# Handing out an attention kernel's side work in smaller portions, one step apart

## The chip, the cores and the metric

The kernel runs on one NeuronCore of a Trainium2 chip as one program in one launch. The metric is the device time in microseconds (us); the time of a kernel is the median of its runs. The engines are TensorE (PE; PEld is its weight load), VectorE (DVE), ScalarE (ACT), GpSimd (POOL) and SyncE (SP), which issues most of the DMAs. All data are fp32.

## The reference

Two layers work on x of 4 images, 32 x 32 tokens, 384 channels. The change lies in layer 0, in its attention and in the routing that follows it. Layer 0, cut to what matters:

```
qkv = layernorm(x) @ qkv_w.T;  q, k, v split into 12 heads of 32
attn = softmax(q @ k.T * 32**-0.5)
gidx = argmax(q @ gp)                  # each token picks one of 48 groups, per head
q_mean = mean of q over each group
tidx = top_k(q_mean @ k, 96)           # per group: its 96 best tokens
col = how many groups of the head chose token m
attn = attn * col;  attn = attn / (attn.sum(over n) + 1e-8)
x = x + (attn @ v) @ proj_w.T
p = softmax(layernorm(x) @ gate_w + gate_b);  the best 2 of 4 experts, weights made to sum to 1
x = x + sum over them of weight * (gelu(layernorm(x) @ w1 + b1) @ w2 + b2)
```

Layer 1 (a local attention over 3 x 3 windows and a feed-forward block) comes after it and is not touched.

## The kernel before

The attention is one long software pipeline. There are 48 heads (4 images of 12) and four steps (u = 0 to 3) a head, so 192 steps; a step treats two tiles of 128 keys against all 1024 queries. The order of the work on PE, DVE, ACT and SP is written out by hand: what Python emits first, an engine runs first. POOL's order is left to the compiler. In each step the loop emits, in this order:

- `scores(u)` (PE, L627) into two PSUM buffers `ps_s`, and `exps` (ACT, L637), which empties them into `e`;
- `out` of eight steps before (PE, L645 into `ps_o`; it needs that step's `wv`), and `total` of one step before (PE, L645 into `ps_z`);
- at u = 0 `gather` of the head before: ACT copies its sums `zr` (L659), SP writes them to DRAM (`z_row`, L661) and reads them back in another layout (`zz`, L663); at u = 3 `keep`: ACT copies a finished head's `po` (L709), SP writes one half over `q` (L718), and POOL's DMA adds the other (`q<-po`, L716);
- `begin` (functions that earlier steps put off with `later`), `widen` (starts a search), for the image before its projection and its routing, the values, then preparation (`prepared`) as far as a budget of 2.6 us a step goes;
- `share` of seven steps before (DVE, L689: two passes over `e` with the row `rz`; then `d` and `wv`, L694 and L696);
- at u = 1 `spread` of the head before: DVE makes `rr` from `zz` (L671, L673), SP writes it (`r_row`, L675) and reads it back to all partitions (`rz`, L677);
- `search()`, `end()`, `search()`: the running searches go on by one portion each time; `end` runs what waits in `ends`, for instance `choose` and a projection's sum;
- at u = 1 the next `Head`: eight DMAs on SP copy its q and k into `q4` and `k4` (L614, L615), which have two buffers each.

The side work is written as Python generators; a `yield` ends a portion. `topk` is the search for the 96th best score of 128 rows: an ACT pass for the size (L366), eight rounds of an ACT pass with Sign (L373) and a new bound by DVE (L377, L379), an exact end by DVE over two halves of the row (L383 to L407), one more Sign (L411) and its use (L413, then `count` one step later). Up to two searches run at once; one starts each 9.4 steps. `prepare` does an image's statistics (BN_STATS, L482 and L483; `std`, L487), normalization, transposes and its q and k. `groups` chooses each token's group (`choose`, L555 and L557), counts the choices (`tally`, ACT, L565) and sums q by group (PE, L589). `prepare` and `groups` yield a cost and a condition; a unit runs once the condition holds. `after(1)` holds from the next step on.

`routed` calculates an image's routing during the next image's heads, one portion a step from its 27th step on; `route` ranks the experts (L1306 to L1325), counts tokens (PE, L1339 and L1340), makes slots and weights (L1342 to L1363) and scatters token numbers into a table (POOL, L1374). After image 2 `router.first` finds the rows of the first four expert blocks, whose weights (L1577) and tokens are then fetched. Image 3's routing and `schedule` run beside the first expert blocks.

Of the kernel before, what the change touches and what calls it, by code (L numbers as in the profile page):

```python
# [23 lines left out]
NH, HD = 12, 32  # L24
# [134 lines left out]
def attention(net, outer, router, x, x1, unsafe, qkv_wT, gpT, proj_wT, proj_w, gate_w, gate_b):  # L159
# [15 lines left out]
    NHEAD = B * NH  # L175
# [8 lines left out]
    with ExitStack() as ctx:  # L184
# [161 lines left out]
        def topk(b, t):  # L346
# [59 lines left out]
            nc.vector.scalar_tensor_tensor(between[:n], last[:n], -(1 - 2.0**-23), none[:n], ALU.mult, ALU.subtract)  # L406
            nc.vector.tensor_scalar(own[:n], hsel[:n, t, :], none[:n], 2.0, ALU.mult, ALU.mult)  # L407
            yield
            over = small("tk_over")
            sign = left.bitcast(BF)[:, :NTOK]  # L410
            nc.scalar.activation(sign[:n], left[:n], AF.Sign, bias=between[:n], accum_out=over[:n])  # L411
# [38 lines left out]
        def prepare(b):  # L450

            im = images[b]
            yield 0, lambda: b == 0 or b - 1 in valued
            xnT = im["xnT"] = early.tile([P, KC, NTOK], FP, name="xnT", tag="xnT")
            for name in ("col", "inv"):
                im[name] = tiny.tile([P, NB, NH], FP, name=name, tag=name, bufs=2)
            nc.gpsimd.memset(im["col"], float(NG))  # L460
            im["mean"] = few.tile([P, NB], FP, name="mean", tag="mean", bufs=3)
            im["std"] = few.tile([P, NB], FP, name="std", tag="std", bufs=3)
            im["z"] = tiny.tile([P, NH, NB], FP, name="zall", tag="zall", bufs=1)
            im["x"] = few.tile([P, NB, NE], FP, name="gate_x", tag="gate_x", bufs=3)

            def turn(xn, o):
                ps = psum()
                for c in range(KC):
                    nc.tensor.transpose(ps[:, c * P : (c + 1) * P], xn[:, c * P : (c + 1) * P], net.ident)
                nc.scalar.copy(xnT[:, :, o : o + P], ps[:, :C].rearrange("p (c t) -> p c t", c=KC))  # L470

            behind = []
            for half in range(2):
                if half and b:
                    yield 0, after(2)
                xt = xts.pop((b, half))
                mv = tiny.tile([P, 4, 2], FP, name="ln_mv", tag="ln_mv", bufs=2)
                rs = tiny.tile([P, 4], FP, name="ln_rs", tag="ln_rs", bufs=2)
                off = tiny.tile([P, 4], FP, name="ln_off", tag="ln_off", bufs=2)
                for t in range(4):  # L480
                    st = tiny.tile([P, 6], FP, name="ln_st", tag="ln_st", bufs=2)
                    nc.vector.bn_stats(st, xt[:, t, :])  # L482
                    nc.vector.bn_aggr(mv[:, t, :], st)  # L483
                    if t % 2:
                        yield 0.3, None
                std = im["std"][:, 4 * half : 4 * half + 4]
                nc.scalar.activation(std, mv[:, :, 1], AF.Sqrt, bias=net.eps["c"])  # L487
                yield 0.3, after(1) if b else None
                nc.vector.tensor_copy(im["mean"][:, 4 * half : 4 * half + 4], mv[:, :, 0])
                nc.vector.reciprocal(rs, std)  # L490
                nc.vector.scalar_tensor_tensor(off, mv[:, :, 0], -1.0, rs, ALU.mult, ALU.mult)
                for two in range(2):

                    yield 1.8, after(1) if b else None
                    while behind:
                        turn(*behind.pop(0))
                    for t in (2 * two, 2 * two + 1):
                        xn = work.tile([P, C], FP, name="xn", tag="xn")
                        nc.scalar.activation(
                            xn, xt[:, t, :], AF.Identity, bias=off[:, t : t + 1], scale=rs[:, t : t + 1]  # L500
                        )
                        behind.append((xn, (4 * half + t) * P))
                if half == 0 and b:
                    fetch(b, 1)
                elif half and b + 1 < B:
                    if b == 0:
                        gating()
                    fetch(b + 1, 0)
            yield 1.8, after(1) if b else None
            while behind:  # L510
                turn(*behind.pop(0))
            for c in range(KC):
                yield 0, lambda: (
                    (b == 0 or len(heads) > NH * (b - 1) + 4 * c + 3)
                    and (b < 2 or len([p for p in projected if p[0] == b - 2]) == NB)
                )
                q = lasting.tile([P, NTOK], FP, name="q", tag="q", bufs=6)
                k = big.tile([P, NTOK], FP, name="k", tag="k", bufs=3)
                im["q"].append(q)
                im["k"].append(k)  # L520
                for out, base in ((q, 0), (k, C)):
                    for half in range(2):
                        yield 2.6, None
                        cols = slice(half * 512, half * 512 + 512)
                        ps = psum()
                        o = base + c * P
                        linear(ps, lambda k: wqkv[:, k, o : o + P], lambda k: xnT[:, k, cols])
                        nc.scalar.copy(out[:, cols], ps)
                reached.add((b, c, "qk"))

        def groups(b):

            im = images[b]
            for c in range(KC):
# [28 lines left out]
                def tally(two, ones_):  # L563
                    one = NB // 2 * (KC * b + c) + two
                    nc.scalar.activation(ones_, ones_, AF.Copy, accum_out=onehot[:, one : one + 1])  # L565
                    chosen.append(two)

                for two in range(NB // 2):
                    yield 0.7, lambda: not ends
# [201 lines left out]
        def routed(b):  # L771
# [24 lines left out]
            yield from router.route(b, logit, im["mv"][:, :, 0], rs)  # L796
            if b == B - 2:
                yield
                router.first()
            if b == B - 1:  # L800
                yield
                yield from router.schedule(late[0])
# [60 lines left out]
        for step in range(STEPS + OUT + 2):  # L863
# [39 lines left out]
            search()  # L903
            end()
            search()
            if u == 1 and n + 1 < NHEAD:
                heads.append(Head(n + 1))
        residue(B - 1, 0)
        assert not ends and not others
# [305 lines left out]
class Router:  # L1215
# [71 lines left out]
    def route(self, b, logit, mean, rs):  # L1287
# [18 lines left out]
        nc.vector.tensor_reduce(one, prob, AX.X, ALU.add)  # L1306
        nc.vector.reciprocal(one, one)
        nc.vector.tensor_tensor(prob, prob, all_(one), ALU.mult)
        pairs = [P, NB, NE, NE]
        ge, gt = self.temp("ge", pairs), self.temp("gt", pairs)  # L1310
        other = prob.unsqueeze(2).to_broadcast(pairs)
        mine = prob.unsqueeze(3).to_broadcast(pairs)
        for t, op, mask in ((ge, ALU.is_ge, self.lower), (gt, ALU.is_gt, self.upper)):
            nc.vector.tensor_tensor(t, other, mine, op)
            nc.vector.tensor_tensor(t, t, mask.unsqueeze(1).to_broadcast(pairs), ALU.mult)
        nc.vector.tensor_tensor(ge, ge, gt, ALU.add)
        sel, at = self.sel[:, tiles, :], self.at[:, tiles, :]
        nc.vector.tensor_reduce(sel, ge, AX.X, ALU.add)
# [24 lines left out]
        nc.vector.tensor_tensor(self.upto[:, b + 1, :], self.upto[:, b, :], pc[:, NE : 2 * NE], ALU.add)  # L1343
        nc.vector.tensor_tensor(base, base, self.region, ALU.add)
        nc.vector.tensor_tensor(at, src, base.unsqueeze(1).to_broadcast(wide), ALU.add)

        part = self.temp("part", wide)
        big = float(2 * NE * NT * P)
# [4 lines left out]
        nc.vector.tensor_scalar(slot[0], slot[0], -1.0, big, ALU.mult, ALU.add)  # L1353
        nc.vector.tensor_tensor(part, at, sel, ALU.mult)
        nc.vector.tensor_reduce(slot[1], part, AX.X, ALU.max)
        there = []
        for n in range(2):
            i = self.temp(f"there_{n}", [P, NB], mybir.dt.int32)
# [23 lines left out]
    def first(self):  # L1382

        nc = self.nc
        shape = [P, NE, self.NJ]
        full = self.temp("full", [P, NE])
        nc.vector.tensor_scalar(full, self.upto[:, B - 1, :], -float(XB), None, ALU.add)
        fills = self.temp("gt", shape)
        nc.vector.tensor_tensor(
            fills, full.unsqueeze(2).to_broadcast(shape), self.steps.unsqueeze(1).to_broadcast(shape), ALU.is_ge  # L1390
        )
        nc.vector.tensor_reduce(full, fills, AX.X, ALU.add)

        self.start = self.pool.tile([P, B + 2, NE], FP, name="rt_start")
        self.begun = self.pool.tile([P, B + 2, NE], FP, name="rt_begun")
        nc.gpsimd.memset(self.begun[:, 0, :], 0.0)
        pre = self.start[:, 0, :]
        nc.gpsimd.memset(pre[:, 0:1], 0.0)
        for e in range(1, NE):
            nc.vector.tensor_tensor(pre[:, e : e + 1], pre[:, e - 1 : e], full[:, e - 1 : e], ALU.add)  # L1400
        taken = self.begun[:, 1, :]
        nc.vector.tensor_scalar(taken, pre, -1.0, float(NFIRST), ALU.mult, ALU.add)
        nc.vector.tensor_scalar(taken, taken, 0.0, None, ALU.max)
        nc.vector.tensor_tensor(taken, taken, full, ALU.min)
        nc.vector.tensor_scalar(taken, taken, float(UNITS), None, ALU.mult)
        nc.vector.tensor_scalar(pre, pre, float(NFIRST), float(UNITS), ALU.min, ALU.mult)
        self.firsts = self.rows(self.pool, "first", NFIRST, 1)

    def rows(self, pool, name, n, groups):
# [883 lines left out]
def metaformer_kernel(  # L2293
# [65 lines left out]
    with tc.If(tc.nc.values_load(unsafe[0:1, 0:1], min_val=0, max_val=1) != 0):  # L2359
        with ExitStack() as outer:  # L2360
# [4 lines left out]
            with ExitStack() as inner:  # L2365
                router = routing(inner)
                for b, given in enumerate(gates(net, router.psum, gate_w, gate_b)):
                    for _ in router.route(b, *given):
                        pass
                    if b == B - 2:  # L2370
                        router.first()
                done = experts(net, router, x1, x2, wup, wdown, router.schedule)
        rest(router, done)

# [58 lines left out]
```

## Time and profile before

| | us |
|---|---|
| median of 3 runs | 2778.15 (2777.52 to 2788.7) |
| the profiled execution's own time | 2777.38 |
| its span, first to last instruction | 2774.9 |

| stretch of the span, us | stage | PE busy | DVE busy | ACT busy | granted clock |
|---|---|---|---|---|---|
| 0 to 80 | loads, first preparation | 54.32 | 14.27 | 30.01 | 1.00 |
| 80 to 1127 | attention, heads 0 to 45 | 962.28 | 757.09 | 793.46 | 0.94 |
| 1127 to 1206 | last heads, end of the pipeline | 51.49 | 52.45 | 24.14 | 0.74 |
| 1206 to 2250 | experts | 1030.15 | 533.18 | 203.76 | 1.00 |
| 2250 to 2775 | layer 1 | 467.21 | 371.29 | 250.49 | 0.94 |

The granted clock is the share of TensorE's full speed that the throttle let through. In a line of waits, the first name is the engine and instruction that stood idle, the name after `<-` is what ended that, and then come the sum in us, the number of times and the longest. A line of the timeline gives the start, the duration, engine, source line, operation and tiles, and in brackets the idle time before it.

### The profile page before, as it was taken

To read this page: it belongs to the slowest core of one execution; us is meant where nothing else is said; L and a number is where in the kernel's file an instruction comes from. 1 tells how busy PE (TensorE), PEld (TensorE's weight loads), DVE (VectorE), ACT (ScalarE), POOL (GpSimd) and SP (SyncE) were. 2 spreads that over 40 slices of the span, in tenths; PEclk is the share of its full clock that TensorE was granted. 3 is DMA by queue.
4 is the path that set the end of the run, shared out by engine and by line. 5 is a ranking of instruction groups with operands and counts; after the bars stand their busy time and mean duration, and the time that the engine had idled before them with its cause. 6 is when DMAs were issued, how large, how long until landed. Compare 5 with 4: busy or idle time off the path is not lost. (4 is left out here: it accounts for less than half of the span.)

```text
span 2774.9 us, 40133 instructions
## 1 busy us (share of the span) xinstructions
PE 2565.5 (92%) x14667; PEld 1558.3 (56%) x14667; DVE 1728.3 (62%) x4362; ACT 1301.9 (47%) x2119; POOL 417.8 (15%) x501
## 2 busy tenths in 40 slices
PE   6889999999999998789999999999999987999988
PEld 3323333333333332247889999999999953555532
DVE  1367778677778787647444544465455556887962
ACT  3778777677778777412221221121121123455455
POOL 1000000030003001413211112222222101110000
PEclk9989999999999998889999999999999999999989
DMA  5133434322322232454665545655655447565532
GB/s 108 33 103 92 108 86 126 95 60 63 96 73 64 59 107 69 133 175 160 230 238 207 202 170 216 232 194 217 237 205 211 175 145 221 165 201 175 173 110 93
DMA packets 215806, 404.13 MB, mean 146 GB/s; under 512 B 83344, under 2 KB 176848, under 8 KB 202544
## 3 DMA queue, kind: packets, MB, share of 16 engines
q1 hardware_dynamic: 184496, 187.82, 22.6%
q0 software_dynamic: 26960, 209.05, 22.0%
q10 hardware_dynamic: 4144, 4.61, 0.5%
q8 instruction: 118, 1.93, 0.3%
q14 instruction: 88, 0.72, 0.1%
HBM read 304.34 MB, written 49.00 MB: 127 GB/s over the span
## 5 line engine op out<-in xcount | busy, mean ns | idle before, releaser
L1702 ACT ACTIVATE h<-ps_h,up 128x256 f32<-128x256 f32 (+1 forms) x420 | 195.1, 465 | 825.3 <-PE ps_h L1697 823.7
L1697 PE MATMUL ps_h<-xbT,up 128*128 128x256 f32 (+1 forms) x2520 | 531.1, 371 | 2.5 <-ACT h L1702 1.8
L689 DVE CUSTOM_DVE_ANT_0 e<-e,rz,inv 128x1024 f32<-128x1024 f32 x384 | 475.3, 1274 | 47.3 <-DMA rz<-r_row 47.3
L1697 PEld LDWEIGHTS ps_h<-xbT,up 128*128 128x128 f32 x2520 | 462.6, 191 | 64.6 <-ACT h L1702 2.6
L637 ACT ACTIVATE e<-ps_s,ten 128x1024 f32<-128x1024 f32 x384 | 408.0, 1109 | 66.6 <-PE ps_s L627 40.1
L627 PE MATMUL ps_s<-q,k 32*128 32x512 f32 x1536 | 297.4, 671 | 51.5 <-ACT e L637 35.0
L645 PE MATMUL ps_o<-e,wv 128*32 128x512 f32 x1536 | 227.2, 666 | 40.3 <-DVE wv L696 38.8
L716 POOL DMA_DIRECT2D q<-po x96 | 76.2, 886 | 947.6 <-DMA q<-po 452.9
L645 PE MATMUL ps_z<-e,rt_ones 128*32 128x512 f32 x1536 | 217.1, 639 | 0.0
L373 ACT ACTIVATE below<-tk_left,tk_bound 128x1024 bf16<-128x1024 f32 (+1 forms) x160 | 184.4, 1152 | 52.4 <-DVE tk_bound L379 41.4
L1741 PE MATMUL ps_y<-wsum,hsum 128*128 128x192 f32 x1116 | 196.0, 329 | 9.5 <-DVE hsum L1657 5.2
L627 PEld LDWEIGHTS ps_s<-q,k 32*128 32x128 f32 x1536 | 92.8, 191 | 189.1 <-ACT e L637 92.0
L1741 PEld LDWEIGHTS ps_y<-wsum,hsum 128*128 128x128 f32 x1116 | 182.5, 191 | 13.2 <-DVE hsum L1657 6.6
L1881 PE MATMUL ps_a<-wa,xnT 128*128 128x486 f32 x384 | 162.1, 571 | 0.6 <-ACT xnT L156 0.6
L1745 DVE TENSOR_TENSOR y<-ps_y,y 128x192 f32<-128x192 f32 x155 | 55.5, 358 | 165.5 <-PE ps_y L1741 162.4
L645 PEld LDWEIGHTS ps_o<-e,wv 128*32 128x32 f32 x1536 | 31.5, 112 | 201.0 <-issue 66.1
L288 PE MATMUL ps_t<-xnT,wqkv 128*128 128x512 f32 x288 | 134.6, 607 | 2.4 <-ACT xnT L470 1.7
L1541 POOL DMA_INDIRECT yt<-yg,index x64 | 78.1, 1220 | 375.5 <-DVE x L1844 181.4
L645 PEld LDWEIGHTS ps_z<-e,rt_ones 128*32 128x32 f32 x1536 | 52.2, 117 | 132.0 <-issue 128.8
L1741 PE MATMUL ps_y<-down,h 128*128 128x192 f32 x744 | 126.0, 326 | 0.0
L1741 PEld LDWEIGHTS ps_y<-down,h 128*128 128x128 f32 x744 | 122.6, 190 | 1.6
L1991 ACT COPY own<-band 128x1040 f32<-128x1040 f32 x96 | 101.7, 1125 | 33.2 <-DMA band<-room 30.8
(398 smaller groups left out, 3576.7 us busy)
## 6 DMA issues: line engine op xcount, KB each, us to landing
band<-room SPq DMA_DIRECT2D x32, 1560.0 KB
rz<-r_row SPq DMA_DIRECT2D x48, 512.0 KB
yg<-y SPq DMA_DIRECT2D x67, 192.0 KB
q<-q SPq DMA_DIRECT2D x192, 64.0 KB
k<-k SPq DMA_DIRECT2D x192, 64.0 KB
room<-none SPq DMA_DIRECT2D x64, 192.0 KB
x<-x SPq DMA_DIRECT2D x35, 192.0 KB
o<-in_x_dram SPq DMA_DIRECT2D x33, 192.0 KB
```

The lines of the kernel that those rows point to most:

```text
L288: nc.tensor.matmul(ps, lhsT=lhsT(k), rhs=rhs(k), start=k == 0, stop=k == KC - 1)
L373: nc.scalar.activation(junk[:n], left[:n], AF.Sign, bias=bound[:n], accum_out=over[:n])
L627: nc.tensor.matmul(ps[:, half * 512 : half * 512 + 512], lhsT=self.k4[r, u * P : (u + 1) * P], rhs=self.q4[r, :], start=True, stop=True,)
L637: nc.scalar.activation(e, ps, AF.Exp, bias=shift, scale=QK_SCALE)
L645: nc.tensor.matmul(ps[r : r + 32, :], lhsT=lhsT(odd), rhs=self.es[2 * u + odd][:, half * 512 : half * 512 + 512], start=u == 0, stop=u == ...
L689: nc.vector.tensor_tensor_reduce(self.es[m], self.es[m], self.rz, 1.0, self.im["inv"][:, m, self.h : self.h + 1], ALU.mult, ALU.add, self. ...
L1541: self.nc.gpsimd.indirect_dma_start(out=y, out_offset=None, in_=self.net.yg[: first_row(self.complete(i // NB)), :], in_offset=bass.Indire ...
L1697: nc.tensor.matmul(ps, lhsT=up[:, o : o + P], rhs=xbT[:, k, :size], start=k == 0, stop=k == KC - 1,)
L1702: nc.scalar.activation(hs[f // 3][:, f % 3, :size], ps, AF.Gelu, bias=up[:, KC * HID + f : KC * HID + f + 1])
L1741: nc.tensor.matmul(ps, lhsT=left[f], rhs=right[:, f, :], start=f == 0, stop=f == HF - 1)
L1881: nc.tensor.matmul(pa[:, :HW_], lhsT=xnTs[i][:, k, :], rhs=wa[:, k, hh * HW_ : (hh + 1) * HW_], start=k == 0, stop=k == KC - 1,)
L1991: nc.scalar.copy(own[:, pairs], m.rearrange("p t (n h) -> p n t h", h=2)[:, pairs])
```

## The change

Nothing is added to or taken from the computation; portions are cut and moved.

1. `topk` yields once more before its last Sign.
2. In `prepare`, for images 1 to 3, two tiles' statistics are one portion, and the next comes in a later step.
3. `tally` reports its choice one step later, so the group sums start one step later.
4. `route` yields four more times, and `router.first` becomes a generator of three portions.
5. The next `Head` is made at the end of step u = 0 if its q and k are there, else at u = 1 as before.

```diff
--- before.py
+++ after.py
@@ -406,6 +406,7 @@
             nc.vector.scalar_tensor_tensor(between[:n], last[:n], -(1 - 2.0**-23), none[:n], ALU.mult, ALU.subtract)
             nc.vector.tensor_scalar(own[:n], hsel[:n, t, :], none[:n], 2.0, ALU.mult, ALU.mult)
             yield
+            yield
             over = small("tk_over")
             sign = left.bitcast(BF)[:, :NTOK]
             nc.scalar.activation(sign[:n], left[:n], AF.Sign, bias=between[:n], accum_out=over[:n])
@@ -482,7 +483,7 @@
                     nc.vector.bn_stats(st, xt[:, t, :])
                     nc.vector.bn_aggr(mv[:, t, :], st)
                     if t % 2:
-                        yield 0.3, None
+                        yield 0.3, after(1) if b else None
                 std = im["std"][:, 4 * half : 4 * half + 4]
                 nc.scalar.activation(std, mv[:, :, 1], AF.Sqrt, bias=net.eps["c"])
                 yield 0.3, after(1) if b else None
@@ -563,7 +564,7 @@
                 def tally(two, ones_):
                     one = NB // 2 * (KC * b + c) + two
                     nc.scalar.activation(ones_, ones_, AF.Copy, accum_out=onehot[:, one : one + 1])
-                    chosen.append(two)
+                    later(lambda: chosen.append(two))
 
                 for two in range(NB // 2):
                     yield 0.7, lambda: not ends
@@ -796,7 +797,7 @@
             yield from router.route(b, logit, im["mv"][:, :, 0], rs)
             if b == B - 2:
                 yield
-                router.first()
+                yield from router.first()
             if b == B - 1:
                 yield
                 yield from router.schedule(late[0])
@@ -903,7 +904,7 @@
             search()
             end()
             search()
-            if u == 1 and n + 1 < NHEAD:
+            if u < 2 and len(heads) == n + 1 < NHEAD and (u or ((n + 1) // NH, (n + 1) % NH // 4, "qk") in reached):
                 heads.append(Head(n + 1))
         residue(B - 1, 0)
         assert not ends and not others
@@ -1306,6 +1307,7 @@
         nc.vector.tensor_reduce(one, prob, AX.X, ALU.add)
         nc.vector.reciprocal(one, one)
         nc.vector.tensor_tensor(prob, prob, all_(one), ALU.mult)
+        yield
         pairs = [P, NB, NE, NE]
         ge, gt = self.temp("ge", pairs), self.temp("gt", pairs)
         other = prob.unsqueeze(2).to_broadcast(pairs)
@@ -1313,6 +1315,7 @@
         for t, op, mask in ((ge, ALU.is_ge, self.lower), (gt, ALU.is_gt, self.upper)):
             nc.vector.tensor_tensor(t, other, mine, op)
             nc.vector.tensor_tensor(t, t, mask.unsqueeze(1).to_broadcast(pairs), ALU.mult)
+        yield
         nc.vector.tensor_tensor(ge, ge, gt, ALU.add)
         sel, at = self.sel[:, tiles, :], self.at[:, tiles, :]
         nc.vector.tensor_reduce(sel, ge, AX.X, ALU.add)
@@ -1343,6 +1346,7 @@
         nc.vector.tensor_tensor(self.upto[:, b + 1, :], self.upto[:, b, :], pc[:, NE : 2 * NE], ALU.add)
         nc.vector.tensor_tensor(base, base, self.region, ALU.add)
         nc.vector.tensor_tensor(at, src, base.unsqueeze(1).to_broadcast(wide), ALU.add)
+        yield
 
         part = self.temp("part", wide)
         big = float(2 * NE * NT * P)
@@ -1353,6 +1357,7 @@
         nc.vector.tensor_scalar(slot[0], slot[0], -1.0, big, ALU.mult, ALU.add)
         nc.vector.tensor_tensor(part, at, sel, ALU.mult)
         nc.vector.tensor_reduce(slot[1], part, AX.X, ALU.max)
+        yield
         there = []
         for n in range(2):
             i = self.temp(f"there_{n}", [P, NB], mybir.dt.int32)
@@ -1390,6 +1395,7 @@
             fills, full.unsqueeze(2).to_broadcast(shape), self.steps.unsqueeze(1).to_broadcast(shape), ALU.is_ge
         )
         nc.vector.tensor_reduce(full, fills, AX.X, ALU.add)
+        yield
 
         self.start = self.pool.tile([P, B + 2, NE], FP, name="rt_start")
         self.begun = self.pool.tile([P, B + 2, NE], FP, name="rt_begun")
@@ -1404,6 +1410,7 @@
         nc.vector.tensor_tensor(taken, taken, full, ALU.min)
         nc.vector.tensor_scalar(taken, taken, float(UNITS), None, ALU.mult)
         nc.vector.tensor_scalar(pre, pre, float(NFIRST), float(UNITS), ALU.min, ALU.mult)
+        yield
         self.firsts = self.rows(self.pool, "first", NFIRST, 1)
 
     def rows(self, pool, name, n, groups):
@@ -2368,7 +2375,8 @@
                     for _ in router.route(b, *given):
                         pass
                     if b == B - 2:
-                        router.first()
+                        for _ in router.first():
+                            pass
                 done = experts(net, router, x1, x2, wup, wdown, router.schedule)
         rest(router, done)
```

The last hunk belongs to a second path, taken only where the first one's method doesn't fit the data; it isn't executed here.

## The prediction

> **What bounds the kernel now.** I read the page's slices first, then busy time and clock by stage, then who waited for whom in the stage of the change, then single stalls in the timeline.
>
> ```profile
> PE   6889999999999998789999999999999987999988
> ACT  3778777677778777412221221121121123455455
> PEclk9989999999999998889999999999999999999989
> ```
>
> Attention fills the first 17 slices. TensorE is at 9 there, but not full, with dips in the clock row. By stage (window, length, PE, PEld, DVE, ACT, POOL busy, granted clock, DMA):
>
> ```profile
> 80.00:1127.00 1047.00, 962.28 (x6172) 335.78 (x6171) 757.09 (x2222) 793.46 (x1212) 123.46 (x136) 0.94 0.32 83
> 1127.00:1206.00 79.00, 51.49 (x303) 12.88 (x299) 52.45 (x143) 24.14 (x27) 18.68 (x20) 0.74 0.40 116
> 1206.00:2250.00 1044.00, 1030.15 (x5497) 941.43 (x5497) 533.18 (x1081) 203.76 (x430) 231.93 (x232) 1.00 0.56 206
> ```
>
> In 80:1127 (nearly all heads) PE is idle for 1047 - 962 = 85 us, and the missing 6% of clock is worth another 0.06 x 1047 = 63 us. So some 148 us lie there beyond PE's own work. The experts stage (99% busy, clock 1.00) leaves nothing. PE's waits in 80:1127 (us, times, longest):
>
> ```profile
> PE ps_s L627 <- ACT e L637: 35.0, 22, 4.7
> PE ps_o L645 <- DVE wv L696: 20.5, 12, 4.6
> PE ps_t L589 <- ACT g L565: 8.8, 8, 1.4
> PE ps_s L627 <- DMA k<-k: 7.5, 9, 2.9
> ```
>
> All waits of that answer make 84.4 us. Why is ACT late with e? In the same window ACT itself waits:
>
> ```profile
> ACT below L373 <- DVE tk_bound L379: 40.9, 27, 6.3
> ACT tk_left L411 <- DVE tk_parts L406: 36.8, 15, 5.8
> ```
>
> One such place in the timeline, and the clock before and after it:
>
> ```profile
> 311.03 1.15 ACT L411 ACTIVATE tk_left<-tk_left,tk_parts 64x1024 bf16<-64x1024 f32 x1 [3.11 <-DVE tk_parts L406]
> 312.18 1.13 ACT L373 ACTIVATE below<-tk_left,tk_bound 128x1024 bf16<-128x1024 f32 x1
> 313.31 2.09 ACT L637 ACTIVATE e<-ps_s,ten 128x1024 f32<-128x1024 f32 x2
> 314.46 3.08 PE L627 MATMUL ps_s<-q,k 32*128 32x512 f32 x8 [2.72 <-ACT e L637]
> 306.50:314.46 7.96, 5.07 (x29) 1.38 (x25) 7.44 (x29) 4.85 (x8) 1.56 (x2) 1.00 0.44 87
> 314.46:321.42 6.96, 6.96 (x33) 1.76 (x34) 3.35 (x10) 5.54 (x7) 0.00 (x0) 0.52 0.24 59
> ```
>
> ACT stands 3.11 us before the search's last Sign (L411), with another Sign and the next two exps queued behind; the exps free the score banks late, and PE stands 2.72 us. Then the clock is 0.52 for 7 us, so those 7 us hold 3.5 us of work. One 3 us wait costs 6 us.
>
> **The change part by part**, against the profiled execution (2777.38 us; span 2774.9).
>
> *Extra yield before the last Sign.* The Sign stood behind DVE's second half of the search (two instructions of 0.7 us, nine small ones); now it goes into the next step, behind that step's exps. No instruction is added. Thirteen PE waits between 99.9 and 1121.0 us follow an L411 wait within 9 us. Taking the smaller of the two each time: 2.2, 2.2, 2.7, 3.2, 1.0, 2.6, 0.8, 0.9, 1.2, 0.7, 0.7, 1.2, 3.0 = 22.4 us. What comes late next is DVE's L413, which now waits in the same step; behind it stands the next step's share (L689). The nearest row is DVE's wait at L377 for a Sign, 63.5 us in 38, so 20 x 1.7 = 34 us of DVE idle time, at 72% busy. Bounds: 0 to 34 x (22.4 / 36.8) = 21 us of PE; I take 0 because few of the L377 waits are followed by a PE wait.
>
> *Statistics in pairs one step apart (images 1 to 3).* Four BN_STATS with aggregation (4 x (0.53 + 0.18) = 2.8 us) lay in one step, now 1.4. Five PE waits follow such a step (1.4 to 3.7 us at 145.4, 176.0, 180.0, 424.9, 459.0): 5 x 1.4 = 7.0 us at most. Preparation ends up to four steps later per image; the steps near 925 us (4.1 us each against a usual 5.7) have no preparation left, so that is covered. Uncovered it would be four steps, 16 us an image.
>
> *Group sums one step after the tally.* The 8.8 us of L589 <- L565 go; PE does a preparation unit instead. If that delays a search, it is by one step of a schedule of 9.4 steps each.
>
> *Routing and first() in pieces.* L1306 to L1325 is 15 DVE instructions, 4.1 us, in one step; L1342 to L1363 is 18, 3.1 us. DVE's share comes behind them and PE's out is due in the next step: waits of 2.6, 1.6, 0.7 and 1.7, 1.7, 4.6 us. Pieces shorten the first burst by 2 us or more, the second by 2.5: 2.0 + 1.6 + 0.7 + 1.7 + 1.7 + 2.5 = 10.2 us. DVE's wait for PE's counts (L1342 <- L1340, 9.5 us) stays. The 16 table scatters (1.26 us each on POOL) move four steps later, past q<-po DMAs; the scatters of 1104 to 1128 already held one up, and ACT waited 1.8 us for it (L709). Bounds -2 to +5 us; I take 0, since as many are passed as before. Image 3's routing runs beside the experts: it needs 27 of the 30 portions that blocks 0 to 2 hand out instead of 23, so its end stays in block 2, at no cost.
>
> *Heads one step earlier.* Eight q/k DMAs on SP (0.6 us of issue each) go before r_row and rz of the head before, and before the x loads and stores of the next step. Their buffers were freed by the scores of the step before, so they wait for nothing new:
>
> ```profile
> 606.89 0.37 SPq L663 DMA_DIRECT2D zz<-z_row  x1
> 609.11 0.33 SPq L675 DMA_DIRECT2D r_row<-rr  x1
> 610.51 0.32 SPq L677 DMA_DIRECT2D rz<-r_row  x1
> 616.16 0.63 SPq L615 DMA_DIRECT2D k<-k  x1
> ```
>
> Gained: the 7.5 us of L627 <- DMA k. Added: the eight issues last from zz at 606.89 + 0.4 to 612.3, so r_row goes 3.2 us later than 609.11. For all 46 heads with this rule, rz (1.45 us behind r_row, landing 4.2 us after issue) would land after DVE's share started in 26 of them, together 44 us; minus the time by which wv was early for PE, 6 us of PE wait stay. Bounds 6 to 44; I take 6, because it is worked out head by head.
>
> *After 1127.* PE stood 8.7 us there for q/k of the last head, because r_row (issued 1145.64) came behind the first expert's weights (issued 1133 and 1143): rz could go only at 1153.12, 7.5 us later instead of 1.4. Now first() ends six steps later, so these weights start some 20 us later and meet the next head's r_row instead. DVE's shares (2.95 us a step, to 1203) bound this end; its 9.0 us wait for rz may go, stay, or come twice: -9 to +6 us, I take 0. The first expert matmul stands at 1208.5, so weights that end near 1173 are hidden; if POOL issued them only behind the last q<-po (1210), that would cost 20 us.
>
> *Sum.* 22.4 + 7.0 + 8.8 + 10.2 + 7.5 = 56 us of the 84.4 us of waits. The clock's 63 us in proportion: 42. Of the 20 stretches at half clock between 80 and 1127, 17 follow one of these waits. Together 98 us. But each stall also let ACT (76% busy) and DVE (72%) catch up: the step at 431.87, after the stall at 424.9, took 2.93 us instead of the usual 5.7. So I keep half, 49 us, with bounds of a quarter and all. Minus 6 us of rz with its clock share, 6 x (1 + 63 / 84) = 10: net 39. 2777.4 - 39 = 2738; the median of the runs is 0.8 us above the profiled execution, so 2739.
>
> The Trainium skill ("TensorE: Matmul & The Clock Gate", Part 1) lets the clock fall only after an idle window of about 3.4 us. By that page only three of these waits (3.7, 4.7 and 4.6 us) would cost clock, and the sum would be 28 - 6 = 22 us of gain, 2756 us. The row at 314.46 shows 0.52 behind a wait of 2.72 us, so the sum above goes by the row.
>
> **The rivals.** *The waits change hands.* ACT's wait at L411 turns into DVE's at L413, and smaller bursts into more steps with a small one; for it speaks that ACT already waits 40.9 us at L373 for DVE. Only the group sums and the q/k loads then keep their worth: 16 - 10 = 6 us, 2771. Against it: the single waits of 2 us and more, which the clock falls after, are the ones that are cut. Chance 0.11.
>
> *SP's order becomes the bound (slower).* Place: DVE's wait for rz, which already makes 34.4 us in 80:1127. If all 44 us came through to PE, each with its clock share, 44 x 1.75 = 77 against 49 gained: 2777.4 + 28 = 2805. It decides from 49 / 1.75 = 28 of the 44 us on. Against it: wv was early for PE by more than 2 us in most heads. Chance 0.10.
>
> *The first weights come too late.* +20 us on the forecast: 2759, still inside its range. The heads' edit may also do nothing for a head whose q/k chunk isn't ready at u = 0; that takes at most its 7.5 us away.
>
> **How the numbers follow.** Forecast 0.79. The range reaches from 2700 (nine tenths of the 98 us kept, less the 10: 78 us of gain) to 2784 (nothing gained, and the tail's +6); it takes in the first rival and leaves out most of the slower one and the rest of the gain. About 0.5%, 14 us, is what a measurement of this kernel can tell from no change: faster 0.79, within it 0.11, slower 0.10.
>
> **What would show it.** Right: ACT L411 <- DVE nearly gone; L589 <- L565 and L627 <- DMA k near zero before 1127; fewer than 20 stretches of half clock and a clock of 0.96 or more there; DVE's wait for rz up from 34 to 60 us or more; first experts' matmul near 1170. Wrong: PE's wait for wv above 20 us, or the clock still at 0.94.

## The result and the profile after

The change makes the kernel slower: 2807.19 us median of 4 runs (2804.69 to 2808.07) against 2780.45 us of 4 runs of the kernel before, ratio 1.009 with a 95% interval of 1.0066 to 1.0114. The profiled execution took 2804.69 us, its span is 2802.8, which is 27.9 us longer than before. Lines from L411 on stand one to seven lower than before: the score matmul is L628, the exps L638, out and total L646, share L690, wv L697.

The same two rows of the slices, then the three stages (window, length, PE, PEld, DVE, ACT, POOL busy, granted clock, DMA):

```profile
PE   6979897899999988769899999999999988899988
PEclk9989999999999998879999999999999999899989
```

```profile
80.00:1127.00 1047.00, 939.60 (x6093) 327.65 (x6095) 737.70 (x2160) 783.02 (x1201) 104.58 (x121) 0.94 0.32 81
1127.00:1206.00 79.00, 48.54 (x325) 13.80 (x321) 52.34 (x157) 32.31 (x34) 32.69 (x32) 0.81 0.41 124
1206.00:2250.00 1044.00, 1013.92 (x5405) 917.27 (x5398) 536.41 (x1101) 197.77 (x418) 235.24 (x233) 0.98 0.56 203
```

The clock in 80:1127 is 0.94 as before, and PE got through fewer matmuls there (6093 records instead of 6172). The first expert matmul stands at 1232.9 instead of 1208.5, so 24 of the 28 us are lost before the experts. Who waited for what in 80:1127 (us, times, longest):

```profile
DVE e L690 <- DMA rz<-r_row: 111.0, 33, 7.5
...
PE ps_o L646 <- DVE tk_parts L377: 33.1, 17, 5.6
...
PE ps_s L628 <- ACT e L638: 25.0, 26, 2.9
...
PE ps_o L646 <- DVE wv L697: 24.4, 10, 6.2
...
DVE topped L414 <- ACT tk_left L412: 18.1, 11, 2.8
...
PE ps_o L646 <- DVE tk_parts L383: 5.3, 2, 4.0
```

The waits that the edits aimed at are gone from the answer: ACT's at L411 (36.8 us before, L412 now), PE's at L589 (8.8) and PE's for k (7.5); PE's wait for e fell from 35.0 to 25.0. In their place PE waits for out's operands: 33.1 + 24.4 + 5.3 = 63 us, where before it was 20.5 + 1.4 = 22. Two of the three rows name tk_parts, an instruction that follows wv on DVE at once; what PE needed there was wv, which ended 0.06 or 0.15 us before out began in every one of these waits. And DVE's wait for rz went to 111.0 us; in the kernel before its line is

```profile
DVE e L689 <- DMA rz<-r_row: 34.4, 19, 6.1
```

One head of the change in the timeline:

```profile
233.55 0.38 SPq L664 DMA_DIRECT2D zz<-z_row  x1
...
234.63 0.57 SPq L615 DMA_DIRECT2D q<-q  x1
...
235.43 0.20 DVE L674 RECIPROCAL rr<-zall 128x8 f32<-128x8 f32 x1
...
240.29 0.63 SPq L616 DMA_DIRECT2D k<-k  x1
...
240.97 0.60 SPq L85 DMA_DIRECT2D room<-none  x1
...
241.67 0.56 SPq L676 DMA_DIRECT2D r_row<-rr  x1
...
243.59 0.34 SPq L678 DMA_DIRECT2D rz<-r_row  x1
...
247.46 1.29 DVE L690 CUSTOM_DVE_ANT_0 e<-e,rz,inv 128x1024 f32<-128x1024 f32 x1 [6.35 <-DMA rz<-r_row]
...
250.64 1.06 PE L646 MATMUL ps_o<-e,wv 128*32 128x512 f32 x8 [0.96 <-DVE tk_parts L377]
```

`rr` is ready at 235.6, r_row goes at 241.67: for 6 us SP works off the eight q and k issues (and one fill of zeros, L85). DVE stands 6.35 us for rz, and PE's out comes just behind wv.

### The profile page after: what moved, and what is told of

It is laid out like the page before. It is cut to its first block, busy times and chain, and to the rows that moved or that the text cites. A ratio compares the mean times of both kernels' runs of the same rounds, so it can differ in the third digit from the quotient of the medians.

```text
span 2802.8 us, 40130 instructions
## 1 busy us (share of the span) xinstructions
PE 2548.8 (91%) x14667; PEld 1551.2 (55%) x14667; DVE 1727.0 (62%) x4362; ACT 1300.9 (46%) x2119; POOL 416.6 (15%) x501
## 5 line engine op out<-in xcount | busy, mean ns | idle before, releaser
L690 DVE CUSTOM_DVE_ANT_0 e<-e,rz,inv 128x1024 f32<-128x1024 f32 x384 | 475.9, 1276 | 134.2 <-DMA rz<-r_row 134.2
L638 ACT ACTIVATE e<-ps_s,ten 128x1024 f32<-128x1024 f32 x384 | 407.0, 1107 | 53.6 <-PE ps_s L628 26.0
L646 PE MATMUL ps_o<-e,wv 128*32 128x512 f32 x1536 | 227.8, 667 | 107.5 <-DVE wv L697 54.9
L628 PE MATMUL ps_s<-q,k 32*128 32x512 f32 x1536 | 272.5, 650 | 25.1 <-ACT e L638 25.0
L646 PE MATMUL ps_z<-e,rt_ones 128*32 128x512 f32 x1536 | 220.9, 647 | 0.0
L646 PEld LDWEIGHTS ps_o<-e,wv 128*32 128x32 f32 x1536 | 32.4, 112 | 263.6 <-issue 138.8
L628 PEld LDWEIGHTS ps_s<-q,k 32*128 32x128 f32 x1536 | 82.4, 186 | 157.6 <-ACT e L638 85.6
L646 PEld LDWEIGHTS ps_z<-e,rt_ones 128*32 128x32 f32 x1536 | 53.9, 118 | 130.0 <-issue 126.7
L1998 ACT COPY own<-band 128x1040 f32<-128x1040 f32 x96 | 101.7, 1127 | 32.3 <-DMA band<-room 29.0
```

The costliest lines, as they stand in the source:

```text
L628: nc.tensor.matmul(ps[:, half * 512 : half * 512 + 512], lhsT=self.k4[r, u * P : (u + 1) * P], rhs=self.q4[r, :], start=True, stop=True,)
L638: nc.scalar.activation(e, ps, AF.Exp, bias=shift, scale=QK_SCALE)
L646: nc.tensor.matmul(ps[r : r + 32, :], lhsT=lhsT(odd), rhs=self.es[2 * u + odd][:, half * 512 : half * 512 + 512], start=u == 0, stop=u == ...
L690: nc.vector.tensor_tensor_reduce(self.es[m], self.es[m], self.rz, 1.0, self.im["inv"][:, m, self.h : self.h + 1], ALU.mult, ALU.add, self. ...
L1998: nc.scalar.copy(own[:, pairs], m.rearrange("p t (n h) -> p n t h", h=2)[:, pairs])
```

## The experiments

The sizes differ between chips: where the kernel before takes 2778 to 2780 us (the result, e13 to e18) edits 1 to 3 bring 1.1%, where it takes 2818 to 2826 us (e1 to e12) 1.75%. So each run is given as a ratio to the kernel before on its own chip, and ratios are compared on one kind of chip. From every trace I also took, for heads 3 to 44, when z_row, r_row, wv and out(0) came. "Chain" is z_row's issue to the end of the first wv, "early" how long before out(0) that is, "tight" the heads where it is under 0.3 us; the columns of time are in us, means over the heads.

| run | kernel | ratio (95%) | r_row after zz | chain | early | tight of 42 | DVE's wait for rz, 80:1127 |
|---|---|---|---|---|---|---|---|
| | before | 1 | 3.8 | 15.9 | 2.9 | 2 | 34.4 |
| | change | 1.009 (1.0066 to 1.0114) | 6.9 | 18.0 | 1.1 | 28 | 111.0 |
| e18 | change without edit 5 | 0.9899 (0.9871 to 0.9927) | 3.4 | 15.4 | 2.5 | 7 | 25.2 |
| e16 | edits 1 to 3 | 0.9888 (0.9865 to 0.9911) | 3.9 | 15.7 | 2.7 | 5 | 33.1 |
| e13 | change, total ahead of out | 1.0118 (1.0103 to 1.0134) | 7.1 | 18.1 | 1.4 | 22 | 113.8 |
| e5 | change, slower chip | 1.01 (1.008 to 1.012) | 7.0 | 18.0 | 1.2 | 28 | 104.5 |
| e1 | without edit 5, slower chip | 0.9849 (0.9813 to 0.9886) | 3.4 | 15.7 | 2.5 | 8 | 24.8 |
| e2 | edit 5 alone | 1.0132 (1.0095 to 1.0169) | 7.0 | 18.2 | 1.6 | 23 | 117.1 |
| e12 | change, only q early | 0.9881 (0.9862 to 0.9899) | 4.4 | 16.4 | 2.0 | 19 | 50.9 |
| e4 | heads at u = 3 | 0.9936 (0.9912 to 0.9961) | 3.1 | 15.3 | 2.0 | 18 | 32.1 |
| e7 | small DMAs between | 1.0197 (1.0174 to 1.0219) | 6.8 | 18.0 | 2.0 | 3 | 103.7 |

**Is it the fifth edit?** e1 undoes it in the change (the diff); e2 makes it alone in the kernel before (the reverse).

```diff
-            if u < 2 and len(heads) == n + 1 < NHEAD and (u or ((n + 1) // NH, (n + 1) % NH // 4, "qk") in reached):
+            if u == 1 and n + 1 < NHEAD:
                 heads.append(Head(n + 1))
```

> The change with its fifth edit undone: the next head's q and k DMAs are issued at u = 1 again, behind r_row and rz. Theory 1 (SP's order): DVE's wait for rz in 80:1127 falls from 111.0 us back to 30 to 50 us, PE's waits that end with wv (33.1 + 25.0 or so of PE ps_o in the changed kernel) fall under 20 us, and the attention is shorter than before: 2740 to 2770 us. Rival (the waits only change hands, from L411 to DVE's L414 and ACT's L373): the time stays at 2775 to 2800 and PE is idle for 80 us or more in 80:1127, under other names.

> The kernel before with the fifth edit alone: the next head's q and k DMAs are issued at the end of u = 0. Theory 1 (SP's order): DVE's wait for rz goes from 34 us in 80:1127 to 90 us or more, part of it comes through to PE, and the time is 2790 to 2810 us. Rival (the edit is worth its q/k waits, the loss is elsewhere): rz at 50 us or less, PE's 7.5 us of DMA waits gone, 2765 to 2778 us. By my own forecast it was 6 us of rz against 7.5 us of q/k: 2775 to 2780.

e1: 0.9849, e2: 1.0132, and e5, the change on such a chip:

> The change itself, beside the three runs that follow, so that each can be set against it on one chip. Its ratio to the kernel before was 1.009; the fifth edit undone gave 0.985. If the fifth edit costs 2.4% as these two say, this run is 2.0 to 2.8% longer than the change without it.

e5 gave 1.010, so the fifth edit costs 1.010 / 0.9849 = 2.5% (2.0 to 3.1). Without it DVE's wait for rz is 24.8 us; alone it makes 117.1. PE, without the fifth edit (e1) and with it alone (e2), in 80:1127:

```profile
PE ps_s L628 <- ACT e L638: 28.7, 26, 3.8
PE ps_o L646 <- DVE wv L697: 10.8, 7, 3.4
...
PE ps_o L646 <- DVE tk_parts L377: 4.4, 5, 1.8
```

```profile
PE ps_o L645 <- DVE tk_parts L377: 33.5, 13, 6.5
...
PE ps_o L645 <- DVE wv L696: 22.0, 14, 3.1
```

Theory 1 holds in both, and both go a little beyond its ranges (by these ratios 2736 and 2815 us where the kernel before takes 2778, and e1's wait for rz under 30). The rival, that the waits only change hands, would have left e1 at no gain. The two runs also show that the edits don't add up: without the fifth edit, edits 1 to 4 bring 1.5% (e1, 1.1 to 1.9), beside it only 1.010 / 1.0132, 0.3% (-0.2 to 0.9).

**SP's issue time, or the data?** e7 takes the change without its fifth edit and puts eight DMAs of a few numbers between zz and r_row.

```diff
+    def dummies(self):
+        for r in range(4):
+            rows_ = slice(32 * r, 32 * r + 32)
+            nc.sync.dma_start(out=few_q[rows_, :], in_=self.q4[rows_, :4])
+            nc.sync.dma_start(
+                out=few_k[rows_, :].rearrange("p (a t) -> p a t", t=4),
+                in_=self.k4[rows_, :].rearrange("p (a t) -> p a t", t=P)[:, :, :4],
+            )
...
+            if u == 0 and n + 1 < NHEAD and ((n + 1) // NH, (n + 1) % NH // 4, "qk") in reached:
+                heads[n].dummies()
             if u == 1 and n + 1 < NHEAD:
```

> The change without its fifth edit (ratio 0.985), and at the end of each u = 0 eight DMAs of 32 partitions on SP that move only 4 or 4 x 4 numbers of a row into tiles nobody reads; the next head's own q and k DMAs stay at u = 1. So there is extra work on SP between zz and r_row, and no q or k moved earlier. Theory 1 (the time that SP takes to issue eight DMAs delays r_row): DVE's wait for rz in 80:1127 rises from 24.8 us to 80 us or more, ratio 1.00 to 1.015. Rival (the loss comes from the q and k data in flight beside r_row, or from their early arrival): the wait stays below 50 us, ratio 0.985 to 0.992.

The median of these issues is 0.597 us (4 numbers a row) and 0.628 us (4 x 4), those of the real q and k in the same trace are 0.597 and 0.627: the bytes don't count, the issue does. The wait for rz rose to 103.7 us:

```profile
DVE e L701 <- DMA rz<-r_row: 103.7, 32, 7.4
...
PE ps_s L639 <- DMA k<-k: 28.2, 20, 4.8
```

So the wait for rz comes from SP's time ahead of r_row. What PE pays for it e7 doesn't show. The ratio, 1.0197, is above what I expected and is no measure of the rz delay: the real q and k now follow still later, PE waits 28.2 us for k, only 3 heads have wv as their tight end, and PE's waits at out are 35.6 us up to the experts, less than the 44.7 of e1. The Trainium skill ("Trainium Kernel Development and Optimization", Key Constraints) says that issuing from several engines "only saves the sequencer's issue time". The trace doesn't contradict that, but here this time, 8 x 0.61 = 4.9 us a head on SP, is what makes r_row late.

**Half of it, and one step earlier.** e12 issues only the four q DMAs at u = 0 (`Head` issues q, `keys` the four k DMAs), e4 all eight at the end of u = 3 of the head before, ahead of z_row.

```diff
                 heads.append(Head(n + 1))
+            if u == 1 and n + 1 < NHEAD:
+                heads[n + 1].keys()
```

> The change with half of its fifth edit: the four q DMAs at the end of u = 0, the four k DMAs at u = 1 behind r_row and rz. All eight early gave 1.010 and 105 to 111 us of DVE's wait for rz in 80:1127; none early gave 0.985 and 24.8 us. Theory 1 (r_row is late by the time of the issues ahead of it, and PE has little slack): in between, rz at 45 to 75 us, ratio 0.992 to 1.003. Rival (the loss has a threshold, and four issues still fit beside zz's own flight of 2 to 4 us): rz at 35 us or less, ratio 0.983 to 0.988.

```diff
+                m = n + 2 if u == 3 else n + 1
+                there = (m // NH, m % NH // 4, "qk") in reached
+                if u != 2 and len(heads) == m < NHEAD and (u == 1 or u == 3 and there):
+                    heads.append(Head(m))
```

> The change with the next q and k DMAs issued one step earlier still, at the end of u = 3 of the head before, so that they stand ahead of z_row and zz and not between zz and r_row. Theory 1 (SP's order between zz and rz is what costs): DVE's wait for rz in 80:1127 falls from 111.0 to 50 us or less and the q/k waits stay gone, 2745 to 2775 us. Rival (any eight issues ahead of the head's sums delay it as much, since SP has no room): rz stays at 90 us or more and the time at 2800 us or more.

e12's wait for rz is 50.9 us, inside theory 1's range, but its ratio of 0.9881 lies at the rival's edge: of the 2.5% half the issues cost 0.3% (-0.2 to 0.9). Half the issues are not half the delay. `rr` is ready 3.4 us after zz's issue, and four issues nearly fit into that time: r_row comes 1.0 us later than in e1 (4.4 against 3.4 us after zz), with eight 3.5 us later. PE's waits at out(0) of heads 3 to 44 rise from 8.7 to 18.4 us, with eight (e5) to 59.3. A cost in proportion to the delay would be 0.7%, which the interval doesn't exclude. In e4 DVE's wait for rz is back at 32.1 us, but zz now comes late (28.8 us in e1):

```profile
DVE zall L672 <- DMA zz<-z_row: 60.4, 25, 10.2
...
DVE e L690 <- DMA rz<-r_row: 32.1, 15, 4.7
```

0.9936 against 0.9849 for e1: eight issues ahead of the head's sums cost there too, about a third of what they cost between zz and r_row. Theory 1 has the wait for rz right and didn't name the one for zz; its range of times, set for a kernel before of 2778 us, holds the ratio (2760).

**A loop through PE's order?** In PE's order out(0) of one head comes ahead of total(3) of the next, whose z_row follows. I thought that this closes a loop, and put total first at u = 0.

```diff
+            if u == 0 and 0 <= step - 1 < STEPS:
+                heads[(step - 1) // PAIRS].total((step - 1) % PAIRS)
             if 0 <= step - OUT < STEPS:
                 heads[(step - OUT) // PAIRS].out((step - OUT) % PAIRS)
-            if 0 <= step - 1 < STEPS:
+            if u and 0 <= step - 1 < STEPS:
                 heads[(step - 1) // PAIRS].total((step - 1) % PAIRS)
```

> The change, with total(3) of a head put ahead of out(0) of the head before it in PE's order at u = 0 (in the kernel before and in the change out comes first, so that a head's sums, and with them its z_row, wait for the out(0) that waits for the last head's rz). Theory 1b (the loop): z_row, zz, r_row, rz, share, out(0) and the next head's z_row form a loop of one head's length, 18.3 + 4.4 us in the change; where it fills the 22.9 us of a head, each late rz is paid in full and head after head. With total first the return from out(0) to z_row leaves the loop: fewer than 15 of 42 heads with wv ready less than 0.3 us ahead of out(0) (28 in the change), ratio 0.985 to 1.000 against 1.010. Rival 1a (only lateness: r_row is 3 us late and each head loses what its slack doesn't cover, whatever the order on PE): 25 heads or more, ratio 1.005 to 1.012.

> The kernel before with the same order on PE, as a control: 2 of 42 heads are tight there. Theory 1b: the order alone is worth little where the loop has slack, 0.995 to 1.001. If it gives 0.985 or less, the order is worth much by itself and a gain in the change doesn't speak for the loop.

> Edits 1 to 3 (ratio 0.9825) with the same order on PE. Theory 1b: 5 of 42 heads are tight there, so little is left to win by it, 0.978 to 0.983; a version that could beat both kernels. Rival: total, put first, makes out and the next scores later and costs as much as it brings, 0.983 to 0.990.

The loop falls as the cause of the loss: e13 is 1.0118, no faster than the change. Its 22 tight heads lie between the two forecasts. Its waits of PE at out fell (22.7 + 19.8 us in the two largest rows), but PE's wait for e rose from 25.0 to 34.0. e15, the control, is 1.0004. e14 gave 0.9926 (0.9909 to 0.9943); set beside the same without that order, on one chip:

> Edits 1 to 3 again, beside the same with total first and beside the change without its fifth edit, on one chip. On the second chip, where the kernel before took 2818 to 2826 us, edits 1 to 3 gave 0.9825; with total first, on a chip where before took 2778 us, 0.9926. If the order on PE costs the difference, this run is 0.980 to 0.985 and some 1% faster than its neighbour e17; if the chip makes it, the two are within 0.3% of each other.

> Edits 1 to 3 with total first, as before: 0.990 to 0.995 if the order on PE costs 1%; within 0.3% of e16 if it costs nothing.

> The change without its fifth edit again, on the chip of e16 and e17: it gave 0.985 on the second chip. If the gain of edits 1 to 4 is the same on every chip, 0.981 to 0.989; if it depends on the chip as e16 may show, it stays within 0.4% of e16.

e16 0.9888, e17 0.9914 (0.989 to 0.9938), e18 0.9899: total first brings nothing, and by these runs the larger gains of e1 and e6 belong to their chips. On this kind of chip the fifth edit costs 1.009 / 0.9899 = 1.9% (1.4 to 2.5), 53 us. e16, at 2748.09 us, and e18, at 2750.8, beat both kernels; their intervals overlap.

**The other edits.** Routing and first() as before (e3), edits 1 to 3 (e6), image 2's routing two portions a step (e8), and the first three edits one by one.

```diff
-                yield from router.first()
+                router.first()
```

This is e3, with the four yields of `route` and the two of `first` gone too. e6 is that and e1's edit together. e8 adds to e1:

```diff
                 next(routing[b - 1], None)
+                if b == B - 1:
+                    next(routing[b - 1], None)
```

> The change with its fourth edit undone: routing and first() in the portions of before, so the scatters and the first weights' issues stand six steps earlier again. Theory 2 (the end of the attention pays for later first weights and scatters): r_row of the last head but one no longer stands behind weight loads, the PE waits of 5.8 and 13.3 us in 1127:1230 fall to 5 us or less together, and the time is 2790 to 2800 us, 8 to 16 us below the change. Rival (the smaller portions of the routing save what the forecast gave them, 10 us, and the end is as long either way): 2807 to 2820 us.

> The first three edits alone (search, statistics, group sums); routing, first() and the heads as in the kernel before. With the heads as before, the fourth edit is then told by this run against the change without the fifth edit (ratio 0.985). My forecast gave the routing's smaller portions 10 us of PE waits, so this should be 0.988 to 0.990. Theory 2 (the end pays for late first weights): 0.981 to 0.983, because first() comes six steps earlier. If both hold they cancel and the ratio is 0.985.

> The change without its fifth edit, and image 2's routing handed out two portions a step, so that its first() ends some nine steps earlier, in the gap between rz of heads 44 and 45, and the first expert's weights are loaded there. Theory 2: the 12 us of PE's wait in the last heads goes, first expert matmul 10 to 15 us earlier, ratio 0.979 to 0.982. Rival (the weights collide with some head's rz or q and k wherever they are put): 0.984 to 0.988.

e9, e10 and e11 put one line each into the kernel before: `topk`'s second `yield`, `after(1) if b else None` after two statistics, and this one in `tally`:

```diff
-                    chosen.append(two)
+                    later(lambda: chosen.append(two))
```

> The kernel before with the first edit alone (one more step before the search's last Sign). Edits 1 to 3 together gave a ratio of 0.9825. My forecast's terms were 22.4 us (search), 7.0 (statistics) and 8.8 (group sums); shared out in proportion the search alone should give 0.989 to 0.991. Rival (the wait only changes hands, from ACT's L411 to DVE's L413): 0.997 to 1.001.

> The kernel before with the second edit alone (two tiles' statistics a step). In proportion to its 7.0 us: 0.996 to 0.998. If a later end of the preparation is not covered, as I priced it at up to 16 us an image: 1.005 or more.

> The kernel before with the third edit alone (group sums one step after the tally). In proportion to its 8.8 us: 0.995 to 0.997, and PE's wait at L589 for ACT's L565 gone. Rival (a search that starts one step later costs what the wait gave): 0.999 to 1.003.

| run | ratio (95%) |
|---|---|
| e3, change without edit 4 | 1.0039 (1.0022 to 1.0055) |
| e6, edits 1 to 3 | 0.9825 (0.98 to 0.9851) |
| e8, without edit 5, routing twice a step | 0.984 (0.98 to 0.988) |
| e9, edit 1 alone | 0.9951 (0.9934 to 0.9967) |
| e10, edit 2 alone | 0.9938 (0.9921 to 0.9956) |
| e11, edit 3 alone | 0.9907 (0.9887 to 0.9927) |

Beside the fifth edit the fourth costs 1.010 / 1.0039 = 0.6% (0.2 to 1.0); without the fifth it is worth nothing that can be told (e6 against e1, e16 against e18). By its ratio e3 lies at the lower end of theory 2's range (about 2790 us), but PE's longest wait at the end is still 5.7 us. The traces of e16 and e18 show where its gain went: e18 starts step 187 at 1100.3 us, e16 at 1116.5, but the first expert matmul stands at 1168.7 and 1178.9, and the spans are 2742.1 and 2741.4. PE's largest waits among the first expert blocks, e16 and e18:

```profile
PE ps_y L1742 <- DVE hsum L1658: 4.2, 1, 4.2
```

```profile
PE ps_y L1748 <- DVE hsum L1664: 8.2, 1, 8.2
PE ps_t L1627 <- DVE xb L1617: 3.2, 2, 2.5
```

So 16 us are won inside the attention, 6 given back in the last heads and some 7 in the first expert blocks (first to last expert matmul 1024.0 and 1031.1 us). The last heads, in the change:

```profile
1180.94 1.04 POOL L1584 DMA_INDIRECT up<-in_wup_dram,rows_w_first  x1 [1.63 <-PE ps_s L628]
...
1182.29 0.99 POOL L1584 DMA_INDIRECT down<-in_wdown_dram,rows_w_first  x1 [0.30 <-issue]
...
1184.49 0.33 SPq L676 DMA_DIRECT2D r_row<-rr  x1
...
1194.82 0.32 SPq L678 DMA_DIRECT2D rz<-r_row  x1
...
1202.71 1.93 PE L646 MATMUL ps_o<-e,wv 128*32 128x512 f32 x8 [13.26 <-DVE wv L697]
```

rz can go only 10.3 us after r_row, which stands behind the weight loads, and PE waits 13.3 us. In e18 the loads go at 1113.8 and 1116.0, and the zz of head 46 between them (1115.7) is late instead: DVE waits 12.9 us for it, and PE 11.6 us behind DVE. In e8 the weights go some nine steps earlier, and DVE waits 12.3 us for the zz of head 44 behind them, with a PE wait of 7.2 us at 1127.9. So at each of the places tried they met some head's chain. e8's interval holds the edges of both its forecasts.

## Why the prediction was wrong

I forecast 2739 us and faster at 0.79; it is slower. Of the rivals it is the second, SP's order, that came. That its time (2805) is so close to the measured 2807 is partly luck: it set 77 us of loss against 49 of gain, the runs show 53 (the fifth edit) against 28 (e18), and both errors cancel.

**The step that failed is the heads' edit**: "minus the time by which wv was early for PE, 6 us of PE wait stay. Bounds 6 to 44; I take 6". Both numbers were too small. For heads 3 to 44 DVE's wait for rz rose by 80 us (34.4 to 114.5), not by 44, and PE's wait at out(0) by 58 (5.5 to 63.8), not by 6. Against e18, on the same kind of chip, PE's waits from the first scores to the first expert matmul are 151.2 us instead of 94.3, so 57 us more; of them 63 at out (107.5 against 44.6), less what it waits less for scores. The clock took another 25 us (85.0 against 59.6 us of full clock lost). The two overlap, and the stretch is 1152.3 against 1088.0 us, 64 us longer. I had priced the edit at 10 us of loss, and 7.5 us of q/k waits with their clock share as gain; the runs say 53 us of loss net.

**What was mis-sized in it is rz's lateness.** The 3.2 us were read at one head, where r_row stood only 2.2 us behind zz; they put r_row 5.4 us behind zz. The mean in the change is 6.9 us: zz's own issue 0.4, the eight q and k issues 5.0, 1.3 other issues (zeros, x loads and stores) 0.8, and gaps between issues 0.8; I had the first two alone. And rz followed r_row by 2.1 us on the mean, where I had 1.45. With r_row 5.4 us behind zz, my rule gives 43 us of lateness and 6 us at PE for heads 3 to 44 of the kernel before, as in the prediction. With each head's distance from zz to rz in the change (9.0 us on the mean) put into the same rule and the same trace, it gives 106 and 37 us; on e18's trace, where edits 1 to 4 are made, 119 and 47. So 2 us more for each rz make the PE wait six times as long, because only what is above a head's slack counts, and most of the 58 us were to be had from the subtraction itself. The same rule with e12's times, on e1's trace, gives 3 us, where 10 were measured. These are estimates worked out from the traces (for DVE's wait the rule gives too much, 106 where it rose by 80); the rest of PE's rise, 10 to 20 us, stays open.

A mean of the slack tells little here: in the kernel before wv was 2.9 us early on the mean and the chain grew by 2.1 us, yet in 19 of the 42 heads wv was less than 2.4 us early; in the change 28 are tight. Edits 1 to 4 take some of this slack away: in e18 it is 2.5 us on the mean, and 26 heads lie under 2.4. That fits their small gain beside the fifth edit (0.3% against 1.5%), but it is not the main cause, since e2, which lacks these edits, loses 1.3% too. That a loop through PE's order closes the delay falls with e13.

**Right: the first three edits.** My sum has 22.4 + 7.0 + 8.8 = 38.2 us of wait for them, with clock and the half kept 38.2 x 98 / 56 / 2 = 33 us. e16 measures 1 - 0.9888 = 1.12%, 31 us (25 to 38). That the sum fits is in part luck. On the slower chips it is 1.75%, 49 us (e6), and the split over the three was wrong: alone, on such a chip, the search brought 14 us (my share 20), the statistics 17 (6) and the group sums 26 (8). Their sum, 2.0%, can't be told from e6's 1.75%. Why the group sums bring more than their 8.8 us of wait is open. The first rival, that the waits change hands, is partly true of the search: in 80:1127 of e9 (on its slower chip) PE waits 20.7 us instead of 35.0 for e, but 26.5 instead of 20.5 for wv, and DVE waits 19.8 us for the last Sign.

**Routing: 9 us forecast, none measured.** The gain inside the attention is there, 16 us to step 187, but "its end stays in block 2, at no cost" was wrong by 7 us (e18 against e16; that the longer routing beside the first blocks makes PE wait for hsum there is argued, not isolated), and the end of the attention ("-9 to +6 us, I take 0") came out at the bad end: from step 187 to the first expert matmul it is 68.4 us in the change, 61.9 before.

**The signs I named.** L411, L589 and the wait for k: gone, right. DVE's wait for rz of 60 us or more: right, and the sign to look at. Fewer than 20 half-clock stretches and a clock of 0.96: 25 and 0.94, wrong; e18 has 18 and 0.96. First expert matmul near 1170: 1232.9, wrong; in e18 1168.7. Both signs of being wrong came: PE's wait for wv is above 20 us (24.4 in the line that names wv) and the clock still 0.94. The signs were thus those of the change without its fifth edit; its time, 2751 us, is still 12 above the forecast.

## What to carry to other kernels

A latency chain that every iteration runs once (here sums to DRAM and back, DVE, TensorE) is to be kept free of issues on its queue: in these runs an issue cost its time in the queue however few bytes it moved. What counts is how far the issues reach beyond the time in which the chain waits anyway: four put r_row 1.0 us later and eight 3.5 us, and the eight cost 1.9 to 2.5%. Where a delay is set against slack, take both iteration by iteration: the mean hides the iterations that have little, and a delay read off one of them, here 2 us too short, made the remainder six times too small. And edits that shorten work ahead of a hand-over also move what the hand-over starts: look at the stage behind it before the gain is booked.

## What the runs showed of the hardware

- In e7 an issue on SP took 0.597 us (median) for 32 rows of 4 numbers and as long for 32 rows of 512; zz and rz, with 128 partitions on the SBUF side, took 0.37 and 0.33.
- A small r_row behind two indirect weight loads landed so late that rz went 10.3 us after it, instead of some 2; in e18 it was a zz between them, for which DVE waited 12.9 us.
- The chips differ by up to 1.7% on the kernel before (2778 to 2826 us), and the gain of edits 1 to 3 by more than its interval (0.9825 on one, 0.9888 on another); why the slower one gains more is open.
